# The LSTM's second step on row pairs by seven products instead of eight, and a longer stated time for the norm behind layer 2

## The chip, the cores and the metric

The kernel runs on one core of one Trainium2 chip. The metric is device time in microseconds (us) of one execution, as the median of several runs. TensorE (PE in the profile; PEld is its loading of weights), VectorE (DVE), ScalarE (ACT), GpSimd (POOL) and SyncE (SP, here only a queue that issues DMAs) each work through a list of instructions of their own, in the order in which the program was built.

## The reference

The input `x` is 128 graphs of 64 nodes with 256 features. Four graph layers follow one another, each as `x = layernorm(x + layer(x))`. Cut to what matters:

```
layer 0:  three times  adj^2 (elementwise) @ (h @ W), relu between
layer 1:  U @ (relu((U.T @ x) @ W1 + b1) @ W2 + b2),  U the eigenvectors of adj's Laplacian
layer 2:  h = relu(adj @ (x @ Wg0 + bg0));  h = relu(adj @ (h @ Wg1 + bg1))
          for p in 1..4:
              windows of p successive nodes; an LSTM with weights Wih[p-1], Whh[p-1] over each window
              h at the window's last node = last hidden state
layer 3:  attention over the graph's edges:  softmax(mask(h h^T)) h + b,  h = x W + b_lin
```

One LSTM step is

```
g = x_t @ Wih.T + h @ Whh.T + bias          # gates i, f, g, o of 256 each
c = sigmoid(f) * c + sigmoid(i) * tanh(g);  h = sigmoid(o) * tanh(c)
```

For p = 2 there are 32 windows in a graph and two steps. The first step has no `h` yet. The second step is what the change rewrites.

## The kernel before

**Tiles and groups.** The 8192 rows (graph and node) make 64 tiles of 128 rows, held in one buffer `X` of 64 x 256 floats in each of 128 partitions. Four tiles are a group: 8 graphs, 512 rows, 16 groups. Everything is fp32. A product of fp32 operands appears in the profile as two TensorE instructions, each with its loading of weights.

**Two phases.** Phase one runs layer 0 for all groups, two at a time; the eigenvectors of layer 1 are computed beside it on VectorE. All of `X` is loaded at the start through SP's queue. A list `norms` holds the single steps of layer 0's norm, which are handed out one after each product. Phase two (from about 860 us) runs layers 1, 2 and 3 group by group, three groups at a time (`WAYS = 3`), each at a different place.

**The order in phase two.** Only TensorE's order is laid out by hand. Every stage is a generator that issues a burst of products and yields the time from which its next burst may come. `now` is a clock that `mm` moves on by a stated time for each product. The loop at the end of the kernel takes the oldest group whose time has come; if none has, it sets `now` to the earliest time. The stated times are constants: `NORM = 5.2` behind a norm, `CELL[256] = 3.8` behind an LSTM step with 256 columns, `CONV`, `MOVE` and `SOFT` elsewhere. They wait for nothing; they only decide in which order the bursts stand. VectorE's, ScalarE's and GpSimd's orders come from the framework's scheduler. All four engines then go through their lists in order, and semaphores hold back an instruction whose operand isn't there.

**Around the change.** In `lstm` (L989 to L1057) the hidden states of layer 2 are held transposed, features in partitions, in `hT` (a buffer named `w` in the profile), with columns of 8 graphs x 64 nodes. A step at p = 2 has 8 units, two halves of 128 features for each of the gates f, i, g, o. A unit of the second step is four products of 256 columns, two with `wih` (L716, `w,wih`) and two with `whh` (`hs,whh`), added in one PSUM bank. ScalarE reads the bank with bias and tanh into `gates` (L1030). VectorE makes the cell (L1034, L1036, L1038), ScalarE its tanh (L1039), and VectorE stores the result into `hT` (L1051), or into `hs` (L1041) when another step follows. The weights of a sigmoid are folded into tanh with a factor of a half.

When `lstm` for p = 4 has ended, `layer2` turns the result back (L926, `ident,w`), adds it to `X` (L1096) and calls `norm`: statistics on VectorE (L551, L552), the root on GpSimd (L553, L554), the scaling on VectorE (L564). It is called for two tiles at a time. Layer 3 then turns `X` (L926, `ident,X`), multiplies by `dw`, turns the result (L926, `ident,w`), makes the scores (L1146), the exponentials on ScalarE (L1159), and turns them (L926, `ident,att`). A copy on ScalarE (`eT`, L1166) is the operand of the last products (`w,v`); VectorE adds them to `X` (L1176), and a norm and the output's DMA (L1184) follow. Layer 1 uses `u2`, `bw1`, `ut2` and `bw2` as weights and L965, L971, L986 on VectorE. Layer 2's mixing and its two products are `adT2`, `cw0`, `cw1`, with copies L953 (VectorE), L954 (ScalarE) and the addition L1067.

The last two groups (`ENDING`) are handled apart: their norms are scaled on ScalarE, and their layer 3 goes in halves.

Of the kernel before, what the change touches and what calls it, by code (L numbers as in the profile page):

```python
# [533 lines left out]
P = 128  # L534
# [3 lines left out]
ENDING = (14, 15)  # L538
LEAD = 10


def norm_parts(tc, pool, x, half, scalar=False):

# [53 lines left out]
def kernel(  # L597
# [48 lines left out]
        nc.sync.dma_start(t, src.rearrange(pattern, **kw))  # L646
        return t

    X = keep.tile([P, NT, D], F32, name="X")
    adst = keep.tile([P, N], F32, name="adst")  # L650
    eig_c = ea.tile([P, len(CONSTS), N], F32, name="eig_c")
    nc.scalar.dma_start(adst[:N, :], adj)
    nc.sync.dma_start(adst[N:, :], adj)
    nc.scalar.dma_start(X[:, 2:4, :], x_t[:, 2:4, :])
    for t in range(2):
        nc.sync.dma_start(X[:, t, :], x_t[:, t, :])
    aw1 = load(wa, "aw1", a_w1, "(k p) f -> p k f", [P, 2, 512], p=P)
    aw2 = wa.tile([P, 4, 1024], F32, name="aw2")
    for h in range(2):
        cols = slice(h * 512, (h + 1) * 512)  # L660
        nc.sync.dma_start(aw2[:, :, cols], a_w2.rearrange("(k p) f -> p k f", p=P)[:, :, cols])
    aw3 = load(wa, "aw3", a_w3, "(k p) f -> p k f", [P, 8, D], p=P)
    for t in range(4, NT, 2):
        nc.sync.dma_start(X[:, t:t + 2, :], x_t[:, t:t + 2, :])
    nc.sync.dma_start(eig_c, consts)

    ident = keep.tile([P, P], F32, name="ident")
# [74 lines left out]
            yield now[0] + 0.3  # L742

    def layer0(g):
        xs = X[:, 4 * g:4 * g + 4, :]

        def mixed(dst, src, nf, more, then=None):
            for c in range(nf):
# [105 lines left out]
        for t in (2, 0):  # L854
            p = tl(psa, [P, 2, D], "ps", bufs=6)
            mm(p, sqT2, s3[:, t:t + 2, :])
            yield now[0]
            x2 = xs[:, t:t + 2, :]
            VL.tensor_add(x2, p, x2)
            norms.extend(scalar_norm(tc, small, x2, half, spare))  # L860

# [48 lines left out]
    for i in range(4):  # L912
        wih.append(load(wb, f"wih{i}", c_ih[i], "(k p) f -> p k f", [P, 2, 1024], p=P))
        whh.append(load(wb, f"whh{i}", c_hh[i], "(k p) f -> p k f", [P, 2, 1024], p=P) if i else None)
    att = []
    for i in range(WAYS):
        att.append(wb.tile([P, 4, P], F32, name=f"att{i}"))
# [44 lines left out]
    def layer1(xs, ready):  # L962
# [25 lines left out]
            yield now[0]  # L988
        return ready  # L989

    def lstm(hT, p, first, nw):

        n = 8 * nw
        wi, wh, bias = wih[p - 1], whh[p - 1], cbi[:, p - 1, :]
        c = hs = None
        for t in range(p):
            rows = slice(first + t, first + t + (nw - 1) * p + 1, p)
            xt = [hT[:, k, rows, :] for k in range(2)]  # L1000
            last = t == p - 1
            names = "figo" if t else "igo"
            G = tl(pg, [P, 2048], "gates")[:, :2 * len(names) * n].rearrange("p (q h n) -> p q h n", h=2, n=n)
            gate = {q: G[:, i] for i, q in enumerate(names)}
            units = [(h, q) for h in range(2) for q in names]

            ahead = {}
            early = units[:2] if t else []
            for h, q in early:
                m = slice(("ifgo".index(q) * 2 + h) * P, ("ifgo".index(q) * 2 + h + 1) * P)  # L1010
                ahead[h, q] = pp = ps4()[:, :n]
                for k in range(2):
                    mm(pp, wi[:, k, m], xt[k], k == 0, False)
            if t:
                yield ready
            if p > 1 and not t:
                c = tl(pg, [P, 512], "c")[:, :2 * n].rearrange("p (h n) -> p h n", h=2)
            new = None if last else tl(pg, [P, 512], "hs")[:, :2 * n].rearrange("p (h n) -> p h n", h=2)
            for h, q in units:
                j = 2 * "ifgo".index(q) + h  # L1020
                m = slice(j * P, (j + 1) * P)
                pp = ahead.get((h, q))
                if pp is None:
                    pp = ps4()[:, :n]
                    for k in range(2):
                        mm(pp, wi[:, k, m], xt[k], k == 0, k == 1 and not t)
                if t:
                    for k in range(2):
                        mm(pp, wh[:, k, m], hs[:, k, :], False, k == 1)
                S.activation(gate[q][:, h, :], pp, AF.Tanh, bias=bias[:, j:j + 1], scale=0.5 if q == "g" else 0.25)  # L1030
                if q == "g":
                    to = gate["g"][:, h, :] if t or p == 1 else c[:, h, :]
                    if t:
                        V.scalar_tensor_tensor(c[:, h, :], gate["f"][:, h, :], 1.0, c[:, h, :], op0=ALU.add,  # L1034
                                               op1=ALU.mult)
                    V.scalar_tensor_tensor(to, gate["i"][:, h, :], 1.0, gate["g"][:, h, :], op0=ALU.add, op1=ALU.mult)  # L1036
                    if t:
                        V.scalar_tensor_tensor(c[:, h, :], c[:, h, :], 0.5, to, op0=ALU.mult, op1=ALU.add)  # L1038
                    S.activation(gate["i"][:, h, :], c[:, h, :] if p > 1 else to, AF.Tanh, scale=0.5)  # L1039
                if q == "o" and not last:  # L1040
                    V.scalar_tensor_tensor(new[:, h, :], gate["o"][:, h, :], 1.0, gate["i"][:, h, :], op0=ALU.add,  # L1041
                                           op1=ALU.mult)
                if q == "o":
                    if h == 0:
                        yield now[0]
                elif h == 1 or len(units) == 8:
                    yield now[0]
            if last:

                for h in range(2):  # L1050
                    V.scalar_tensor_tensor(hT[:, h, slice(first + p - 1, first + nw * p, p), :],  # L1051
                                           gate["o"][:, h, :].rearrange("p (w b) -> p w b", b=8), 1.0,
                                           gate["i"][:, h, :].rearrange("p (w b) -> p w b", b=8), op0=ALU.add,
                                           op1=ALU.mult)
            ready = now[0] + CELL[n]
            hs = new
        return ready  # L1057

    def layer2(xs, g, ready):
        a = yield from mixed(xs, adT2, ready)  # L1060
        g1 = as3(work(), 4)
        ready = []
        for t in range(0, 4, 2):
            p = ps4((P, 2, D))
            for j in range(2):
                run(p[:, j, :], [(a[:, k, (t + j) * P:(t + j + 1) * P], cw0[:, k, :]) for k in range(2)])
            V.tensor_add(g1[:, t:t + 2, :], p, wide["c_b0"].unsqueeze(1).to_broadcast([P, 2, D]))  # L1067
            relu(g1[:, t:t + 2, :], g1[:, t:t + 2, :])
            ready.append(now[0] + CONV)
            yield now[0]  # L1070
        a = yield from mixed(g1, adT2, ready)
        hT = tl(pw, [P, 1024], "w").rearrange("p (k n b) -> p k n b", k=2, b=8)
        for c in range(2):
            p = ps4((P, 4, P))
            run(p, [(cw1[:, k, c * P:(c + 1) * P], a[:, k, :]) for k in range(2)])
            h = work2()
            V.scalar_tensor_tensor(as3(h, 4), rs_row.unsqueeze(1).to_broadcast([P, 4, P]), cb1[:, c:c + 1], p,
                                   op0=ALU.mult, op1=ALU.add)
            S.activation(hT[:, c, :, :].rearrange("p n b -> p b n"), as3(h, 8), AF.Relu, scale=2.0)
            yield now[0]  # L1080
        ready = now[0] + CONV
        for p, first, nw in ((1, 0, 32), (1, 32, 32), (2, 0, 32), (3, 0, 21), (4, 0, 16)):
            if first == 0:
                yield ready
            ready = yield from lstm(hT, p, first, nw)
        hb = as3(work(), 2)
        V.tensor_copy(as3(hb[:, 0, :], 8), hT[:, 0, :, :].rearrange("p n b -> p b n"))
        S.copy(as3(hb[:, 1, :], 8), hT[:, 1, :, :].rearrange("p n b -> p b n"))
        yield ready + 1.6
        ready = []  # L1090
        for t in range(0, 4, 2):
            p = ps4((P, 2, D))
            for j in range(2):
                for k in range(2):
                    turn(p[:, j, k * P:(k + 1) * P], hb[:, k, (t + j) * P:(t + j + 1) * P])
            V.scalar_tensor_tensor(xs[:, t:t + 2, :], p, 0.5, xs[:, t:t + 2, :], op0=ALU.mult, op1=ALU.add)  # L1096
            norm(xs, t, ready, 1.8 if t and g in ENDING else 0.0, scalar=g in ENDING)
            yield now[0]
        return ready

# [84 lines left out]
            yield now[0]  # L1185

    def group(g):
        xs = X[:, 4 * g:4 * g + 4, :]
        ready = [0.0, 0.0]
        ready = yield from layer1(xs, ready)  # L1190
        ready = yield from layer2(xs, g, ready)
        if g in ENDING:

            mine = next(x for x in going if x[3] == g + 1)
            going.append([ready[1], mine[1] + 1, layer3(xs, g, ready, 2, 2), g + 1])
            yield from layer3(xs, g, ready, 0, 2)
        else:
            yield from layer3(xs, g, ready, 0, 4)

# [60 lines left out]
```

## Time and profile before

| | |
|---|---|
| median of 10 runs | 2539.27 us (2537.01 to 2541.73) |
| the profiled execution's own time | 2537.25 us |
| its span, first to last instruction | 2535.5 us |
| granted TensorE clock, mean | 0.997 |
| TensorE busy | 2490.7 us, 15020 instructions |
| VectorE busy | 1410.2 us, 4996 instructions |
| ScalarE busy | 1096.1 us, 2706 instructions |
| GpSimd busy | 133.1 us |
| second-step products at p = 2 with `whh` (128x256) | 512 instructions |
| VectorE busy in 0 to 800 us / 900 to 1000 us / 1000 to 2300 us | 641.6 / 31.3 / 604.2 us |

A busy time is a sum over the instructions of an engine; the profiled time is a little longer than the span, since it takes in what lies around the first and last instruction. The profile gives every instruction its line in the kernel, its output and its operands; products issued through `mm` all have the line L716, and so are told apart by their operands' names. A time of a TensorE product in the timeline ends with the model of its pipeline, so that neighbouring rows overlap; the distance of the starts says how fast products follow one another. In a table by stretches of time the columns are the stretch, its length, the busy time and number of instructions of PE, PEld, DVE, ACT and POOL, the granted clock, the share of DMA and GB/s.

### The profile page before, as it was taken

How to read it: one execution, taken by the hardware profiler on the slowest of the kernel's cores; microseconds unless marked ns; L12 is line 12 of the kernel's file. 1: busy time of each engine (PE TensorE's matmuls, PEld its weight loads, DVE VectorE, ACT ScalarE, POOL GpSimd, SP SyncE). 2: the span in 40 equal slices, each digit the busy share in tenths (PEclk: the TensorE clock that was granted, in tenths of full speed). 3: DMA queues.
4: the chain of work that ended last, by engine and by line, in shares of the span. 5: the costliest groups of instructions: out<-in, count | busy, mean ns of one | idle time of the engine just before them, and what ended most of it. 6: DMA issues, size and time to landing. Idle time of an engine off the chain costs nothing.

```text
span 2535.5 us, 38990 instructions
## 1 busy us (share of the span) xinstructions
PE 2490.7 (98%) x15020; PEld 2188.2 (86%) x15020; DVE 1410.2 (56%) x4996; ACT 1096.1 (43%) x2706; POOL 133.1 (5%) x316
## 2 busy tenths in 40 slices
PE   9999999999999999999999999999999999999997
PEld 7788887888877889998989889898898988988996
DVE  6888777778885433454453544535445444353235
ACT  2344433434333354445444454443444444445444
POOL 0000000000000100000000000000000000010001
PEclk9999999999999999999999999999999999999998
DMA  6000000000000300000000000000000000000000
GB/s 220 1 1 1 1 1 1 1 1 1 1 1 1 117 1 1 9 9 1 9 9 1 9 1 9 9 1 9 1 9 9 1 9 5 5 9 1 1 1 26
DMA packets 24634, 32.09 MB, mean 13 GB/s; under 512 B 2176, under 2 KB 21376, under 8 KB 24448
## 3 DMA queue, kind: packets, MB, share of 16 engines
q1 hardware_dynamic: 24096, 29.32, 3.4%
q8 instruction: 118, 1.93, 0.3%
q14 instruction: 68, 0.56, 0.1%
q10 hardware_dynamic: 352, 0.28, 0.0%
HBM read 21.20 MB, written 8.39 MB: 12 GB/s over the span
## 4 chain that ended last, share of the span: by engine, by line
PE 92%; DVE 5%; POOL 1%; issue 1%; DMA 1%; ACT 0%; SPq 0%; ACTq 0%; POOLq 0%; DVEq 0%
PE ps L716 89%; PE ps L926 2%; POOL ln_rs L554 1%; DVE D L51 1%; DVE X L564 1%; DVE X L1096 1%; PE ps L1146 1%; DVE ln_st L551 1%; PE pc L93 1%; DMA X<-in_x_dram 1%; DVE tw L51 0%; POOL ln_rs L553 0%; DVE ln_mv L552 0%; DVE h L51 0%; DVE u L51 0%
## 5 line engine op out<-in xcount | busy, mean ns | idle before, releaser
L716 PE MATMUL ps<-w,wih 128*128 128x256 f32 (+2 forms) x4992 | 895.3, 319 | 0.0
L716 PEld LDWEIGHTS ps<-w,wih 128*128 128x128 f32 x4992 | 761.3, 191 | 54.1 <-issue 12.7
L1030 ACT ACTIVATE gates<-ps,cbi 128x128 f32<-128x128 f32 (+2 forms) x1248 | 502.7, 410 | 574.1 <-PE ps L716 567.0
L716 PE MATMUL ps<-hs,whh 128*128 128x128 f32 (+2 forms) x3072 | 539.7, 303 | 0.8 <-DVE hs L1041 0.8
L716 PEld LDWEIGHTS ps<-hs,whh 128*128 128x128 f32 x3072 | 453.0, 191 | 17.2 <-issue 1.7
L1036 DVE SCALAR_TENSOR_TENSOR gates<-gates 128x256 f32<-128x256 f32 (+2 forms) x256 | 89.5, 349 | 294.6 <-ACT gates L1030 294.6
L716 PE MATMUL ps<-aw,h 128*128 128x256 f32 x1024 | 227.2, 379 | 0.0
L716 PEld LDWEIGHTS ps<-aw,h 128*128 128x128 f32 x1024 | 192.9, 190 | 25.9 <-ACT h L725 0.5
L725 ACT ACTIVATE h<-h 128x512 f32<-128x512 f32 x128 | 80.6, 629 | 169.4 <-DVE h L51 169.2
L1039 ACT ACTIVATE gates<-c 128x128 f32<-128x128 f32 (+2 forms) x288 | 98.0, 340 | 94.0 <-DVE c L1038 83.4
L1034 DVE SCALAR_TENSOR_TENSOR c<-gates,c 128x128 f32<-128x128 f32 (+2 forms) x192 | 62.6, 326 | 117.8 <-ACT gates L1030 117.5
L716 PE MATMUL ps<-ss,tw 128*128 128x256 f32 x512 | 117.9, 380 | 0.0
L716 PE MATMUL ps<-ss,aw 128*128 128x256 f32 x512 | 117.3, 379 | 0.0
L716 PE MATMUL ps<-m,aw 128*128 128x256 f32 x512 | 117.1, 380 | 0.0
L716 PE MATMUL ps<-aw,m 128*128 128x512 f32 x256 | 114.5, 593 | 0.0
L1041 DVE SCALAR_TENSOR_TENSOR hs<-gates 128x128 f32<-128x128 f32 (+2 forms) x192 | 62.7, 327 | 89.2 <-ACT gates L1039 51.6
L564 DVE TENSOR_SCALAR X<-X,ln_mv,ln_rs 128x256 f32<-128x256 f32 x176 | 64.8, 410 | 81.0 <-POOL ln_rs L554 81.0
L1051 DVE SCALAR_TENSOR_TENSOR w<-gates 128x256 f32<-128x256 f32 (+2 forms) x160 | 59.5, 378 | 90.2 <-PE ps L716 61.0
L716 PEld LDWEIGHTS ps<-ss,aw 128*128 128x128 f32 x512 | 96.6, 190 | 12.8
L716 PEld LDWEIGHTS ps<-ss,tw 128*128 128x128 f32 x512 | 96.3, 190 | 12.9 <-issue 0.2
L553 POOL TENSOR_SCALAR ln_rs<-ln_mv 128x2 f32<-128x2 f32 x96 | 25.4, 264 | 1555.7 <-DVE ln_mv L552 1555.3
L716 PEld LDWEIGHTS ps<-m,aw 128*128 128x128 f32 x512 | 95.6, 190 | 12.6 <-issue 0.5
(294 smaller groups left out, 3089.3 us busy)
## 6 DMA issues: line engine op xcount, KB each, us to landing
X<-in_x_dram SPq DMA_DIRECT2D x30, 256.0 KB, 6.0
out_dram<-X SPq DMA_DIRECT2D x28, 256.0 KB, 2.1
wih<-in_c_ih_dram SPq DMA_DIRECT2D x4, 1024.0 KB, 7.2
aw<-in_a_w_dram SPq DMA_DIRECT2D x3, 1024.0 KB, 10.3
whh<-in_c_hh_dram SPq DMA_DIRECT2D x3, 1024.0 KB, 9.3
out_dram<-X SPq DMA_DIRECT2D x8, 128.0 KB, 1.7
aw<-in_a_w_dram SPq DMA_DIRECT2D x1, 512.0 KB, 5.8
cw<-in_c_w_dram SPq DMA_DIRECT2D x2, 256.0 KB, 5.1
```

The source lines that it names most:

```text
L51: return getattr(self.engine, name)(out, *args, **kw)
L553: nc.gpsimd.tensor_scalar(rs, mv[:, :, 1], EPS, None, op0=ALU.add)
L564: nc.vector.tensor_scalar(x[:, t, :], x[:, t, :], mv[:, t, 0:1], rs[:, t:t + 1], op0=ALU.subtract, op1=ALU.mult)
L716: PE.matmul(out, lhsT, rhs, start=start, stop=stop)
L725: S.activation(dst, src, AF.Relu)
L926: PE.transpose(out, in_, ident)
L1030: S.activation(gate[q][:, h, :], pp, AF.Tanh, bias=bias[:, j:j + 1], scale=0.5 if q == "g" else 0.25)
L1034: V.scalar_tensor_tensor(c[:, h, :], gate["f"][:, h, :], 1.0, c[:, h, :], op0=ALU.add, op1=ALU.mult)
L1036: V.scalar_tensor_tensor(to, gate["i"][:, h, :], 1.0, gate["g"][:, h, :], op0=ALU.add, op1=ALU.mult)
L1039: S.activation(gate["i"][:, h, :], c[:, h, :] if p > 1 else to, AF.Tanh, scale=0.5)
L1041: V.scalar_tensor_tensor(new[:, h, :], gate["o"][:, h, :], 1.0, gate["i"][:, h, :], op0=ALU.add, op1=ALU.mult)
L1051: V.scalar_tensor_tensor(hT[:, h, slice(first + p - 1, first + nw * p, p), :], gate["o"][:, h, :].rearrange("p (w b) -> p w b", b=8), 1.0, ...
```

## The change

It has three parts.

1. **The norm behind layer 2** is given a stated time that is longer by 1.3 for all groups but the last two.
2. **The second step at p = 2** goes through a new function `second`. The 32 windows are split into two halves of 16, the 256 input features (partition halves) and the 1024 gate rows into two each, and the 2 x 2 block product is made from seven block products by Strassen's scheme in Winograd's form, once with `wih` and `xt` and once with `whh` and `hs`, both added in the same place in PSUM. `less` makes four combinations of the moving operand for each of `xt` and `hs` on VectorE; `add_weights` makes four combinations of each weight once, in the first group. A product P1 to P7 is two units (`q`) of 128 columns, 4 TensorE products each; two products P share a PSUM bank. ScalarE copies P1 to `u1`, and VectorE adds the others into the four blocks a, b, c12 and d of the gates. ScalarE then applies bias and tanh from there, two windows' halves in one instruction, and the stores into `hT` come at the end of the step's function, four pieces of 128 columns in place of two of 256.
3. **Room for the sums.** The two buffers of weight sums take 16 KB in each partition. `X` is cut to 48 tiles. The last four groups go through layer 0 first. Their rows are stored in DRAM (`rest`) when their norm is done, and the space is loaded with the rows of groups 0 to 3. When groups 0 to 3 have left layer 3, the stored rows are loaded back. The store and the two loads are one more entry in the list `norms` for each of the four groups.

```diff
@@ load, layer0 @@
-    X = keep.tile([P, NT, D], F32, name="X")
+    X = keep.tile([P, NT - 4 * LATE, D], F32, name="X")
+    rest = [aside.tile([P, 4, D], F32, name=f"rest{i}") for i in range(LATE)]
+    order = list(range(NT // 4 - LATE, NT // 4)) + list(range(NT // 4 - LATE))
...
+        def change():
+            nc.sync.dma_start(rest[g], xs)
+            for t in (0, 2):
+                nc.sync.dma_start(xs[:, t:t + 2, :], given(order[g + LATE])[:, t:t + 2, :])
...
+        if g < LATE:
+            norms.append(change)
@@ weights @@
+    def add_weights():
+        for w, s in zip((wih[1], whh[1]), sums):
+            a11, a12, a21, a22 = quarters(w)
+            V.tensor_add(s[:, 0], a21, a22)
+            V.tensor_sub(s[:, 1], s[:, 0], a11)
+            V.tensor_sub(s[:, 2], a11, a21)
+            V.tensor_sub(s[:, 3], a12, s[:, 1])
@@ new: second @@
+    def second(hT, xt, hs, G, c, bias, ready):
+        def less(s, b1, b2, part):
+            T = [both[:, s, i].rearrange("p (w b) -> p w b", b=8) for i in range(4)]
+            if 0 in part:
+                V.tensor_sub(T[0], b1[1], b1[0])
+            if 1 in part:
+                V.tensor_sub(T[2], b2[1], b1[1])
+                V.tensor_sub(T[1], b2[1], T[0])
+                V.tensor_sub(T[3], b2[0], T[1])
...
+        less(0, x1, x2, (0, 1))
+        less(1, h1, h2, (0, 1))
...
+        moving = ((x1[0], h1[0]), (x2[0], h2[0]), (x2[1], h2[1]), T4, T1, T2, T3)
+        weight = (0, 1, 6, 2, 3, 4, 5)
+        yield ready
+        for h in range(2):
...
+            def two(*which):
+                p = ps4((P, 2, 2, P))
+                for at, i in enumerate(which):
+                    for q in range(2):
+                        for s in range(2):
+                            mm(p[:, at, q, :], ways[s][weight[i]][:, q, h, :], moving[i][s], s == 0, s == 1)
+                return p[:, 0], p[:, 1]
+
+            p1, p2 = two(0, 1)
+            S.copy(u1, p1)
+            V.tensor_add(a, u1, p2)
+            yield now[0]
+            p6, p7 = two(5, 6)
+            V.tensor_add(c12, u1, p6)
+            V.tensor_add(b, c12, p7)
+            yield now[0]
+            p5, p3 = two(4, 2)
+            V.tensor_add(d, b, p5)
+            V.tensor_add(c12, c12, p5)
+            V.tensor_add(c12, c12, p3)
+            p4, _ = two(3)
+            V.tensor_add(b, b, p4)
+            gate = {}
+            for m, q, name in ((1, 0, "f"), (0, 0, "i"), (0, 1, "g"), (1, 1, "o")):
+                j = 2 * "ifgo".index(name) + h
+                gate[name] = G[:, h, :, m, q, :]
+                S.activation(gate[name], gate[name], AF.Tanh, bias=bias[:, j:j + 1],
+                             scale=0.5 if name == "g" else 0.25)
+            ch = c[:, h, :].rearrange("p (w n) -> p w n", w=2)
+            V.scalar_tensor_tensor(ch, gate["f"], 1.0, ch, op0=ALU.add, op1=ALU.mult)
+            V.scalar_tensor_tensor(gate["g"], gate["i"], 1.0, gate["g"], op0=ALU.add, op1=ALU.mult)
+            V.scalar_tensor_tensor(ch, ch, 0.5, gate["g"], op0=ALU.mult, op1=ALU.add)
+            S.activation(gate["i"], ch, AF.Tanh, scale=0.5)
+            yield now[0]
+        for h in range(2):
+            for w in range(2):
+                o, i = (G[:, h, w, m, 0 if m == 0 else 1, :].rearrange("p (w b) -> p w b", b=8) for m in (1, 0))
+                V.scalar_tensor_tensor(hT[:, h, 32 * w + 1:32 * w + 32:2, :], o, 1.0, i, op0=ALU.add, op1=ALU.mult)
+        return now[0] + CELL[256] + 1.0
@@ lstm @@
+            if p == 2 and t:
+                ready = yield from second(hT, xt, hs, G, c, bias, ready)
+                break
@@ layer2 @@
+            elif g == 0:
+                add_weights()
...
-            norm(xs, t, ready, 1.8 if t and g in ENDING else 0.0, scalar=g in ENDING)
+            norm(xs, t, ready, 1.8 if t and g in ENDING else 0.0 if g in ENDING else 1.3, scalar=g in ENDING)
@@ group @@
+        if g < LATE:
+            nc.sync.dma_start(xs, rest[g])
```

## The prediction

> **What bounds the kernel now.** I read the page's busy shares first, then TensorE's list of waits, then two neighbouring groups in the timeline, then the table by stretches. Times are us; in the list of waits the figures are total, times, longest.
>
> ```profile
> PE 2490.7 (98%) x15020; PEld 2188.2 (86%) x15020; DVE 1410.2 (56%) x4996; ACT 1096.1 (43%) x2706; POOL 133.1 (5%) x316
> ...
> PE ps L926 <- DVE X L564: 17.1, 22, 1.1
> ```
>
> TensorE bounds: 98% busy, and its one repeated wait is that of layer 3's transposes (L926) for the norm behind layer 2 (L564), 22 times, so in 11 groups of 16. One such place, TensorE and then VectorE:
>
> ```profile
> 1500.93 1.89 PE L716 MATMUL ps<-w,wih 128*128 128x256 f32 x8
> 1502.65 1.05 PE L716 MATMUL ps<-ut,v 128*128 128x128 f32 x8
> 1504.80 0.67 PE L926 MATMUL ps<-ident,X 128*128 128x128 f32 x4 [1.09 <-DVE X L564]
> 1505.30 1.03 PE L716 MATMUL ps<-bw,v 128*128 128x256 f32 x4
> 1506.80 0.76 PE L926 MATMUL ps<-ident,X 128*128 128x128 f32 x4 [0.47 <-DVE X L564]
> 1507.46 2.86 PE L716 MATMUL ps<-w,wih 128*128 128x256 f32 x12
> ...
> 1569.13 3.73 PE L716 MATMUL ps<-w,wih 128*128 128x128 f32 x32
> 1572.70 1.95 PE L716 MATMUL ps<-bw,w 128*128 128x128 f32 x16
> ```
>
> ```profile
> 1504.24 0.74 DVE L564 TENSOR_SCALAR X<-X,ln_mv,ln_rs 128x256 f32<-128x256 f32 x2 [0.81 <-POOL ln_rs L554]
> 1505.04 0.40 DVE L1036 SCALAR_TENSOR_TENSOR gates<-gates 128x256 f32<-128x256 f32 x1
> 1506.34 0.74 DVE L564 TENSOR_SCALAR X<-X,ln_mv,ln_rs 128x256 f32<-128x256 f32 x2 [0.90 <-POOL ln_rs L554]
> 1506.99 0.75 DVE L1051 SCALAR_TENSOR_TENSOR w<-gates 128x256 f32<-128x256 f32 x2
> ```
>
> A row can be used by its starts: eight instructions of 256 columns take 1502.65-1500.93, 0.215 each; 32 of 128 columns take 1572.70-1569.13, 0.1116 each. The last turn of layer 2 leaves TensorE at 1500.93 and layer 2's next step, the first of row pairs (wih1, 1507.46), starts 6.53 later over 4.36 of products: 2.2 of idle time in a group. And wih1 starts when L1051 has written half of its input (1506.99+0.42). So two things are late together: the norm, and this LSTM input queued behind it on VectorE.
>
> The stretches, columns PE, PEld, DVE, ACT, POOL busy:
>
> ```profile
> 1500.93:1507.46 6.53, 4.97 (x30) 3.84 (x29) 4.82 (x17) 1.95 (x4) 1.92 (x4) 1.00 0.00 0
> 1507.46:1540.52 33.06, 33.06 (x193) 28.02 (x193) 20.98 (x57) 12.60 (x26) 3.92 (x8) 1.00 0.05 17
> 1540.52:1604.00 63.48, 63.48 (x461) 60.27 (x460) 21.44 (x61) 32.50 (x87) 0.00 (x0) 1.00 0.01 1
> ```
>
> VectorE's 56% is a mean over two regimes. In the 39.6 from layer 2's turns to step p=3 (layer 3 of one group, row pairs of the second, layer 1 of the third) it is busy 25.8, and sits six times 0.75 to 1.13 for GpSimd's root; in the 63.5 after that, 21.4.
>
> [...] The rows here have 423 (L971, from PSUM) and 292 (L1041, another operation). [...]
>
> **The change, part by part.** Where instructions stand in the changed program is read from its built order; all durations are from this trace.
>
> *Strassen's products.* Removed per group: 32 fp32 products of 256 columns, two instructions each, 64 x 0.2155 = 13.8. Added: 7 products x 2 x 2 x 2 halves = 56 of 128 columns, 112 x 0.1116 = 12.5. Gain 1.3 a group, 21.0 in 16.
>
> *Its additions.* VectorE gets 14 from PSUM (423 ns) and 8 of 128 columns (292), and the results are stored in 4 pieces of 128 instead of 2 of 256 (+0.3): 5.9+2.3+0.3 = 8.6 busy a group, or 6.4 where nothing depends (rows follow at 0.335 and 0.21). ScalarE gets two copies (0.37 each, L1120's). All 8.6 lies in the busy stretch: 25.8+8.6 = 34.4, with the six waits for GpSimd 40.0, over TensorE's 36.1. Its cover is gone.
>
> *The stated time* (+1.3). In ten groups the order after the turns becomes wih0, ut2, bw2, X turns, wih1 (6 products), X turns. VectorE's order there is unchanged: norm of the first rows, L1036, norm of the second, LSTM input. So wih1 still waits for L1051's place, 6.45 after the turns, with 0.44 less done ahead of it. The wait for L564 should go, and a wait of wih1 for the LSTM input (1.8), with 0.6 of bw2 for ScalarE's copy, takes its place: no gain, 0.44 lost.
>
> *A steady group,* walked from wih1's start (0) by starts and ends of such rows, every engine in its built order:
>
> ```
>  9.9  PE: layer 1's last product done (2.6 wih1 + 0.4 turns + 2.6 wih1 + 3.5 dw + 0.9)
> 13.6  DVE: its add, statistics, 1.15 for GpSimd, norm
> 17.4  DVE: a=u1+P2, two hn adds, scores, c12=u1+P6
> 19.1  DVE: exp on ACT (to 18.4), sums of rows
> 20.4  DVE: b+P7, d=b+P5, c12+P5, b+P4, c12+P3 -> ACT f,i,g,o to 21.85
> 22.8  ACT: second copy of P1, then eT; PE wanted eT at 22.2: waits 0.6
> 31.3  DVE: cell, h, attention added, two norms with 1.1 for GpSimd each
> 31.9  DVE: copy for cw0; PE wanted it at 30.8: waits 1.2
> 32.7  DVE: b, d, c12 of the second half -> ACT to 34.4
> 35.5  DVE: cell, mixed with two layer-1 adds and a copy; ACT tanh to 36.0
> 36.65 DVE: h stored. PE wanted it for p=3 at 33.7: waits 3.0
> ```
>
> Against 33.06 now: +3.6 a group, that is 4.8 of waits, 0.4 of the moved turns, less 1.3 and some rounding. Behind the waiting rows on VectorE stand the norms and adds of the other two groups, and TensorE, in its fixed order, waits for them.
>
> *Elsewhere.* In the first three groups and the last three, 5 to 8 us of other products lie between the last P4 and p=3, or bursts of other steps between the products: I take 1 each for waits, bounds 0 and 3.5 (the steady sum). The sums of weights are 8 operations of 512 columns, 8 x 0.68 = 5.5 on VectorE in the first group, where TensorE is idle 4.1 in 850 to 900: 2 taken, bounds 0 and 5.5. Bank releases: every PSUM bank's eighth predecessor is read before it is wanted.
>
> *Rows kept aside.* SP stores four groups (512 KB each) and loads as much, in layer 0 and again behind the outputs. A 256 KB load lands in 6.0 and a store in 2.1; the store stands behind the norm (about 100 us for the first group, or one group later), and the next reader comes after another group of products, about 50 us. Behind it on SP are only the weights of layer 2, issued 500 us later. The reloads are wanted eight groups later. Cost 0; without that cover some 10 us each.
>
> *Sum:* -21.0 + 10 x 4.9 + 6 + 2 = +36 on the profiled execution's 2537.25: 2573. The median shown is 2.0 above it: **2575**.
>
> **Rivals.**
> - *VectorE keeps up* (faster). If the additions slip into gaps, the 4.8 of new waits vanish and -21+4+6+2 = -9 is left; if the norm's waits also go (11 x 2.2), -37: 2502 to 2530. For it: 56% mean, and at the short spacing the additions are 6.4, not 8.6. Against: six waits for GpSimd block that queue. It decides where the waits of a steady group fall below some 1.2.
> - *Half of it.* With VectorE's chain 2 shorter (dependent rows closer, attention's adds ahead), waits are about 2.8: +16, 2555; with 3.5 shorter, no change.
> - *It spreads.* If the late h delays p=3's first gates and the next norms too, 2 more a group: 2595, up to 2606.
> - *The order change isn't what it says*: the built order shows it made, but a burst moved ahead of a wait has to be ready itself, and wih1 isn't.
>
> **Numbers.** A measurement of this kernel tells about 0.2% (5 us) from no change. Main case 0.62, 2560 to 2590. Half of it 0.11, spreading 0.12, no change 0.05, faster 0.10. The range 2545 to 2606 leaves out the last two and a little above. Slower 0.85.
>
> **What would show it.** Right: waits of L926 for the norm nearly gone; TensorE waiting instead for LSTM inputs (hT) at wih1 and wih2 and for cw0's copy, 60 to 80 in all; VectorE busy near 34 of a stretch of 43; matmul spacing still 0.1116. Wrong: TensorE without waits in p=2 (then the additions were hidden), or waits for DMA or in layer 0.

## The result, and the profile after

| | before | after |
|---|---|---|
| median | 2539.43 us (28 runs) | 2582.46 us (8 runs) |
| ratio, 95% interval | | 1.0169 (1.016 to 1.0178) |
| span of the profiled execution | 2535.5 us | 2579.6 us |
| mean granted clock | 0.997 | 0.992 |

The changed kernel is slower by 43 us; 2575 was predicted. The page's first line of busy times, as shown for the kernel before:

```profile
PE 2490.4 (97%) x15788; PEld 2211.3 (86%) x15788; DVE 1520.1 (59%) x5388; ACT 1097.2 (43%) x2738; POOL 139.7 (5%) x316
```

TensorE has 768 instructions more and is busy as long as before. VectorE has 110 us more; without the wide sums of the weights (5.4) that is 6.5 a group. The time went into TensorE's waits (total, times, longest):

```profile
PE ps L731 <- DVE w L1104: 20.0, 9, 2.2
PE ps L731 <- DVE w L1171: 15.0, 10, 1.5
PE ps L731 <- DVE w L997: 9.3, 10, 1.9
PE ps L731 <- ACT v L1023: 9.1, 12, 1.4
PE ps L731 <- DVE hs L1161: 5.7, 2, 4.9
```

The wait for layer 2's norm (17.1 before) has gone. In its place TensorE waits for the hidden states of p = 2 at the first products of p = 3 (wih2, for L1104), for those of p = 1 at wih1 (L1171), for the copy in front of cw0 (L997) and for ScalarE's copy in front of bw2 (L1023). This is the place behind layer 2's turns, to be read beside the one at 1500.93 in the prediction, TensorE and then VectorE:

```profile
1519.15 1.89 PE L731 MATMUL ps<-w,wih 128*128 128x256 f32 x8
1520.88 1.05 PE L731 MATMUL ps<-ut,v 128*128 128x128 f32 x8
1522.61 1.13 PE L731 MATMUL ps<-bw,v 128*128 128x256 f32 x4 [0.68 <-ACT v L1023]
1523.58 0.60 PE L970 MATMUL ps<-ident,X 128*128 128x128 f32 x4
1525.68 2.86 PE L731 MATMUL ps<-w,wih 128*128 128x256 f32 x12 [1.50 <-DVE w L1171]
```

```profile
1522.46 0.73 DVE L566 TENSOR_SCALAR X<-X,ln_mv,ln_rs 128x256 f32<-128x256 f32 x2 [0.81 <-POOL ln_rs L556]
...
1524.56 0.73 DVE L566 TENSOR_SCALAR X<-X,ln_mv,ln_rs 128x256 f32<-128x256 f32 x2 [0.90 <-POOL ln_rs L556]
1525.21 0.75 DVE L1171 SCALAR_TENSOR_TENSOR w<-gates 128x256 f32<-128x256 f32 x2
```

The turns of `X` find the norm done and start without a wait, but wih1 behind them needs L1171, which still stands behind both scalings and their waits for GpSimd's root. And this is the end of the second step in the same group, all engines, few rows of many:

```profile
1552.62 0.39 PE L731 MATMUL ps<-w,whh 128*128 128x128 f32 x2
...
1553.02 0.74 DVE L566 TENSOR_SCALAR X<-X,ln_mv,ln_rs 128x256 f32<-128x256 f32 x2 [0.75 <-POOL ln_rs L556]
...
1556.02 0.73 DVE L566 TENSOR_SCALAR X<-X,ln_mv,ln_rs 128x256 f32<-128x256 f32 x2 [0.82 <-POOL ln_rs L556]
...
1557.28 0.41 DVE L1086 TENSOR_TENSOR gates<-gates,ps 128x256 f32<-128x256 f32 x1
...
1557.60 0.41 DVE L1088 TENSOR_TENSOR gates<-gates,ps 128x256 f32<-128x256 f32 x1
...
1561.36 0.49 DVE L1104 SCALAR_TENSOR_TENSOR w<-gates 128x128 f32<-128x128 f32 x2
...
1561.91 6.22 PE L731 MATMUL ps<-w,wih 128*128 128x168 f32 x30 [2.22 <-DVE w L1104]
```

The last P4 is done at 1552.85, where TensorE's next row starts. Its addition (L1088) starts 4.75 later, behind layer 3's attention, its norm and two pairs of scalings that waited for GpSimd. Gates, cell and stores follow, and hT is there at 1561.85, 9.0 after P4. The program stated 4.8 for it.

The two stretches of this group (from layer 2's turns to p = 3, and most of the rest; columns PE, PEld, DVE, ACT, POOL busy, then granted clock, DMA share, GB/s):

```profile
1519.01:1561.91 42.90, 37.66 (x274) 32.93 (x272) 33.08 (x98) 14.84 (x33) 5.58 (x12) 1.00 0.04 14
1561.91:1625.61 63.70, 63.70 (x450) 60.70 (x451) 20.33 (x59) 31.26 (x84) 0.00 (x0) 0.97 0.00 1
```

In the first VectorE is busy 33.1 of 42.9 and TensorE 37.7. The second row stops 1.8 short of the next group's wih0, which starts at 1627.42. From wih0 to wih0 the two stretches are 42.8 and 65.5, where the kernel before has 39.6 and 64.0 (1540.52 to 1604.54). In the second TensorE has no wait, but a granted clock of 0.97: a loss of another kind, told below.

**Where the 44.1 of the span lie,** by the starts of the groups' `w,dw` products (once a group):

| from the start of ... | before | after | difference |
|---|---|---|---|
| the span to the 1st group | 1018.3 | 1024.4 | +6.1 |
| 1st to 4th | 284.6 | 293.8 | +9.2 |
| 4th to 13th, nine steps | 932.5 | 964.4 | +31.9 |
| 13th to 14th, with the last groups between | 234.5 | 230.1 | -4.4 |
| 14th to the end | 65.5 | 66.9 | +1.4 |

A step of the nine is 106.6 against 103.6, and 108.3 in three of them.

### The profile page after: what moved, and what is told of

Same layout as the page of the kernel before. It is cut to its first block, busy times and chain, and to the rows that moved or that the text cites. A ratio compares the mean times of both kernels' runs of the same rounds, so it can differ in the third digit from the quotient of the medians.

```text
span 2579.6 us, 41027 instructions
## 1 busy us (share of the span) xinstructions
PE 2490.4 (97%) x15788; PEld 2211.3 (86%) x15788; DVE 1520.1 (59%) x5388; ACT 1097.2 (43%) x2738; POOL 139.7 (5%) x316
## 4 chain that ended last, share of the span: by engine, by line
PE 81%; DVE 12%; POOL 3%; ACT 2%; issue 2%; DMA 0%; SPq 0%; ACTq 0%; POOLq 0%; DVEq 0%
PE ps L731 79%; POOL ln_rs L556 2%; DVE X L566 2%; DVE ln_st L553 2%; PE ps L970 1%; ACT gates L1093 1%; DVE D L51 1%; POOL ln_rs L555 1%; DVE X L1218 1%; DVE ln_mv L554 1%; PE pc L93 1%; DVE w L1262 1%; DMA X<-in_x_dram 0%; DVE X L1298 0%; DVE w L997 0%
## 5 line engine op out<-in xcount | busy, mean ns | idle before, releaser
L731 PE MATMUL ps<-w,wih 128*128 128x128 f32 (+2 forms) x4864 | 848.3, 311 | 35.7 <-DVE w L1104 20.0
L731 PEld LDWEIGHTS ps<-w,wih 128*128 128x128 f32 x4864 | 730.4, 193 | 75.2 <-DVE w L1104 22.3
L1150 ACT ACTIVATE gates<-ps,cbi 128x128 f32<-128x128 f32 (+2 forms) x1120 | 440.7, 403 | 450.7 <-PE ps L731 444.4
L731 PE MATMUL ps<-hs,whh 128*128 128x128 f32 (+1 forms) x2816 | 459.6, 287 | 5.7 <-DVE hs L1161 5.7
L731 PEld LDWEIGHTS ps<-hs,whh 128*128 128x128 f32 x2816 | 397.3, 192 | 9.0 <-DVE hs L1161 6.1
L1156 DVE SCALAR_TENSOR_TENSOR gates<-gates 128x128 f32<-128x128 f32 (+2 forms) x224 | 75.9, 339 | 245.5 <-ACT gates L1150 245.4
L740 ACT ACTIVATE h<-h 128x512 f32<-128x512 f32 x128 | 80.5, 629 | 183.9 <-DVE h L51 183.8
L1161 DVE SCALAR_TENSOR_TENSOR hs<-gates 128x128 f32<-128x128 f32 (+2 forms) x192 | 62.7, 327 | 93.9 <-ACT gates L1159 58.9
L731 PE MATMUL ps<-w,sums 128*128 128x128 f32 x896 | 114.1, 276 | 0.0
L1159 ACT ACTIVATE gates<-c 128x128 f32<-128x128 f32 (+2 forms) x256 | 84.5, 330 | 62.7 <-DVE c L1158 48.1
L731 PEld LDWEIGHTS ps<-w,sums 128*128 128x128 f32 x896 | 107.4, 192 | 1.7 <-issue 0.5
L1154 DVE SCALAR_TENSOR_TENSOR c<-gates,c 128x128 f32<-128x128 f32 (+1 forms) x160 | 49.2, 307 | 100.5 <-ACT gates L1150 99.9
```

The costliest lines, as they stand in the source:

```text
L731: PE.matmul(out, lhsT, rhs, start=start, stop=stop)
L740: S.activation(dst, src, AF.Relu)
```

## Experiments

All ratios are to the kernel before on the same chip, with a 95% interval.

### The parts alone

e1, in the kernel before:

```diff
-norm(xs, t, ready, 1.8 if t and g in ENDING else 0.0, ...)
+norm(xs, t, ready, 1.8 if t and g in ENDING else 0.0 if g in ENDING else 1.3, ...)
```

> The kernel before with the norm's stated time longer by 1.3 and nothing else. VectorE's queue is the bound (the theory): the wait for the norm gives place to one of the LSTM input at wih1, no gain and up to 0.44 a group lost in ten groups: 2538 to 2546 against 2539. Rival, the order of bursts does the harm: 2560 or more. Rival, the norm's wait really goes: some 2519 (11 x 1.8 less).

Measured: 2536.63, ratio 0.9990 (0.9983 to 0.9996). A small gain, below the expected range: the groups now come in steps of 107.4 and 98.2 by turns, where both kernels' steps are even but for the clock. TensorE's order is thus another one than the changed kernel's, and e1 doesn't tell what the stated time does in that order.

e2, in the changed kernel, with the norm's stated time of before:

```diff
-            if p == 2 and t:
-                ready = yield from second(hT, xt, hs, G, c, bias, ready)
-                break
```

> The changed kernel with the second step in its old form and the norm's stated time as before: only the rows kept in DRAM and the sums of weights (which nothing reads) are left of the change. Theory: 2 more than before, 2539 to 2544, all of it about 880 to 900 us, where the eight wide additions stand. Rival, the DRAM traffic or the placement costs: 2550 or more, with waits for DMA.

Measured: 2542.67, ratio 1.0008 (1.0002 to 1.0015), some 2 to 3. No wait for the added DMAs. Instead one wait of 4.1 for `w` of L740 at about 890, where the kernel before had 1.2 and 1.4: on VectorE layer 2's first addition stands behind five of the eight wide sums. A stretch of 6.8 at half the granted clock begins at 889, which the kernel before doesn't have. The storing and loading of rows costs nothing that shows.

e5, in the changed kernel, puts the norm's stated time back (the diff of e1 reversed):

> The changed kernel with the norm's stated time of before. If the waits of wih1 (1.5) and of the product behind ScalarE's copy (0.68) come from the longer stated time, they go, and the wait for the norm comes back (1.09 and 0.47 a group): about 0.6 a group less, 2572 to 2582. If the two parts harm each other, clearly less: below 2565. If the norm's waits are longer now that VectorE has more to do: 2585 or more.

Measured: 2548.93, ratio 1.0039 (1.0024 to 1.0054): 33 less than the changed kernel. The outcome is the second of the expectation: **the two parts harm each other.** Alone the stated time gains 3; beside the second step it costs 33. With its old value the second step costs 6 over e2: 27 are lost where 21 are saved. Here too the steps come by turns (108.4 and 98.6 to 101.2), so this one number changed the whole order. And between 900 and 2460 e5 ran 27 us at half the granted clock, some 14 of the 27 that are lost; e2 ran none there (mean granted clock of the profiled executions 0.989 and 0.995).

### Is it VectorE's load?

e3 leaves the additions and the copies of P1 out of the changed kernel; the gates are read from the banks:

```diff
-            S.copy(u1, p1)
-            V.tensor_add(a, u1, p2)
...
-            V.tensor_add(b, b, p4)
...
-                S.activation(gate[name], gate[name], AF.Tanh, ...
+                S.activation(gate[name], (p4 if m else p2)[:, q, :].unsqueeze(1).to_broadcast([P, 2, P]), AF.Tanh, ...
```

> The changed kernel without its 14 additions from PSUM per group and without the copies of P1: ScalarE reads its gates from the banks of P2 and P4 direct, so the values are wrong, all seven products and the eight combinations of the moving side stay. VectorE loses 5.9 of the 8.6 us that it gained. Theory, VectorE: the waits for hT at wih1, wih2 and for cw0's copy mostly vanish, 2500 to 2530. Rival, TensorE's halved products or the order cost it: still above 2560.

Measured: 2539.67, ratio 1.0003 (0.9995 to 1.0012). All of the 43 goes, which speaks against the rival that the halved products or the order do it without the additions, but 2500 to 2530 is missed, and the waits say why:

```profile
PE ps L731 <- DVE w L1161: 15.0, 10, 1.5
PE ps L731 <- ACT v L1023: 8.0, 12, 1.0
PE ps L731 <- DVE w L997: 6.0, 9, 0.7
```

(L1161 here is L1171 of the changed kernel.) The wait at wih2 is gone; in a steady group those at wih1 (1.50) and bw2 (0.68) are what they were, and that for cw0's copy is a little shorter. So the wait at wih2 comes with the additions, and those at wih1 and bw2 don't need them; e9 below shows that they go with another order. The early wait for `hs` (4.9) is there without the additions too. A step is 103.7: the 1.3 saved in products is lost in these.

e4 puts as many additions, into a scratch buffer, into e2, without e2's sums of the weights:

```diff
+            if p == 2 and t:
+                for k in range(8):
+                    V.tensor_sub(extra[:, :P], hs[:, k % 2, :P], hs[:, k % 2, P:])
...
+                if p == 2 and t:
+                    for _ in range(1 + (h == 0 or q in "fi")):
+                        V.tensor_add(extra, hs[:, h, :], pp)
                 S.activation(gate[q][:, h, :], pp, AF.Tanh, ...
```

> The kernel of e2 with its old products (without the sums of weights), and on VectorE 14 additions of 256 columns from the PSUM banks of the second step and 8 of 128 columns, all into a scratch buffer that nothing reads: the load of the change, on nobody's data path. Theory, VectorE's queue: waits of TensorE for hT, for the norm and for copies grow by some 3 to 5 a group, 2570 to 2610. Rival, it is the longer path from the products to the gates (P4 behind two additions) and not the load of the queue: below 2550.

Measured: 2555.92, ratio 1.0065 (1.005 to 1.008), 13 over e2, or some 16 if the 2 to 3 for e2's wide sums are taken off; it lies between the two expectations. One new wait (cw0's copy, 12.0 in 10 times); a step is 105.0. VectorE was as busy as in the changed kernel (1520.4). So in the order of before the load by itself costs 1.4 in a steady group and 13 to 16 in all, about what e5 loses beyond the clock (27 less 14). Whether the rest of the changed kernel's loss comes from its order alone, or also from additions that stand on the way from the products to the gates, e4 can't say: it differs from the changed kernel in both.

e6 takes layer 3's scaling off that queue, in the changed kernel, and e11 does the same in the kernel before:

```diff
-            rows_norm(tc, small, x2, half, ending)
+            rows_norm(tc, small, x2, half, True)
```

> The changed kernel with the scaling of layer 3's norm on ScalarE in all groups, as in the last two. It takes four scalings and two waits for GpSimd's root (0.8 each), 3.1 in all, out of VectorE's queue, just where the additions of the second half stood 4.4 behind the last P4. Theory, these additions wait their turn in that queue: wih2's wait of 2.22 falls below 0.7, and with it the half-clock stretches in the middle go; 2550 to 2562. Rival, the tail from P4 over two additions, four gates and the cell is too long by itself: wih2 still waits 1.5 or more, above 2572.

> The kernel before with the scaling of layer 3's norm on ScalarE: the control for the gain of 27 in the changed kernel. Theory, it is the additions that stand behind these scalings, and the kernel before has none: 2534 to 2542. Rival, a norm off VectorE's queue helps any order: below 2525.

Measured: e6 2555.20, ratio 1.0064 (1.0047 to 1.0081), 27 less than the changed kernel; e11 2540.08, ratio 1.0000 (0.9992 to 1.0009). The same edit is worth 27 where the additions stand behind the scalings and nothing where there are none. The end of the second step in e6, TensorE's last P4 and VectorE, whose other rows are left out:

```profile
1542.29 0.39 PE L731 MATMUL ps<-w,whh 128*128 128x128 f32 x2
```

```profile
1543.30 0.41 DVE L1088 TENSOR_TENSOR gates<-gates,ps 128x256 f32<-128x256 f32 x1
1543.63 0.41 DVE L1086 TENSOR_TENSOR gates<-gates,ps 128x256 f32<-128x256 f32 x1
...
1549.04 0.49 DVE L1104 SCALAR_TENSOR_TENSOR w<-gates 128x128 f32<-128x128 f32 x2
```

P4 ends at 1542.52, and its addition starts 0.8 behind it instead of 4.75; hT is stored at 1549.53, 7.0 after P4, and wih2 waits no more. The rival (the tail is too long by itself) falls: a tail of 7.0 is hidden by the products that lie there. The half-clock stretches between 1130 and 2460 are gone too (mean granted clock 0.995, the changed kernel's 0.992). The price is a new wait for ScalarE's copy in front of cw0 (L998, 11.6 in 10 times), about as long as the one for VectorE's copy that went; a step is 104.7.

e7 moves layer 1's and layer 2's scalings to ScalarE too:

```diff
-            norm(xs, t, ready, 2.0)
+            norm(xs, t, ready, 2.0, True)
...
-            norm(xs, t, ready, ..., scalar=g in ENDING)
+            norm(xs, t, ready, ..., scalar=True)
```

> As the last, with the scalings of layer 1's and layer 2's norms on ScalarE too. VectorE then waits for GpSimd nowhere in the stretch. Theory: the waits at wih1, wih2 and cw0's copy all shrink, 2515 to 2550. Rival, ScalarE takes the place of VectorE (its gates queue behind scalings that wait for the root): above 2560, with waits for ScalarE's outputs.

Measured: 2599.58, ratio 1.0238 (1.0223 to 1.0254). The rival is right here:

```profile
PE ps L731 <- ACT v L1023: 51.1, 12, 5.0
```

ScalarE's copy for bw2 now stands behind scalings that wait for GpSimd, and TensorE waits some 4.8 for that copy in a steady group. Each of these waits in a steady group is followed by 6.8 at half the granted clock, another 3.4 (mean granted clock 0.983). A wait for another engine was paid by what stood behind it, in ScalarE's queue as in VectorE's.

### Is it the order?

e9, in the changed kernel, states 7.0 in place of 4.8, nearer to the 9.0 that the trace shows:

```diff
-        return now[0] + CELL[256] + 1.0
+        return now[0] + CELL[256] + 3.2
```

> The changed kernel with one number changed: the stated time behind the second step, from 3.8 + 1.0 to 3.8 + 3.2. The trace of the changed kernel has 9.0 from the last P4 to the stored hT. The order that is built has the second half of cw0's products ahead of p = 3's first step, and the input products of p = 1 ahead of the turns of layer 2. Theory, the harm is a lack of other products where VectorE is behind, which the order decides: wih2's wait of 2.22 falls by 1.7 or more, and wih1 has its input earlier: 2530 to 2560. Rival, VectorE's load of the stretch is what counts and the waits only move to other bursts: above 2570.

Measured: 2537.84, ratio 0.9991 (0.9983 to 1.0000), **45 less than the changed kernel**, with the same work on every engine. Two rows of TensorE at the turns and three around p = 3:

```profile
1514.28 4.48 PE L731 MATMUL ps<-w,wih 128*128 128x256 f32 x20
1518.60 0.60 PE L970 MATMUL ps<-ident,X 128*128 128x128 f32 x4
...
1547.16 3.72 PE L731 MATMUL ps<-cw,w 128*128 128x256 f32 x16 [0.84 <-DVE w L997]
1550.72 0.45 PE L731 MATMUL ps<-w,wih 128*128 128x168 f32 x2
1551.66 4.54 PE L731 MATMUL ps<-w,wih 128*128 128x168 f32 x30 [0.50 <-DVE w L1104]
```

The second half of cw0's products now lies ahead of p = 3 (16 instructions in place of 8), and wih1 ahead of the turns of `X`. In a steady group the waits at wih1 and bw2 are gone, that at wih2 is 0.5, that for cw0's copy is still 0.84. The last P4 is done at 1542.59, so hT comes about as late as before, some 9 after P4: the longer tail is still there, but products cover it. A step is 102.6.

e10 has the norm's stated time of before and e6's edit:

> The kernel with the norm's stated time of before (2549) and the scaling of layer 3's norm on ScalarE (which took 27 in the other order). Theory, VectorE's queue: the waits for cw0's copy (10.9 in all) shrink, 2530 to 2543. Rival, the order there has its products elsewhere and nothing waits behind layer 3's scalings: 2546 or more.

Measured: 2527.51, ratio 0.9948 (0.9933 to 0.9963), below the expected range: the scalings off the queue are worth 21 in that order too, and the result beats both kernels.

e12 takes e9 and scales layer 3's norm on GpSimd, right behind the root in the same queue, in all groups but the last two:

```diff
-        nc.vector.tensor_scalar(x[:, t, :], ...
+        (nc.gpsimd if pool_scales else nc.vector).tensor_scalar(x[:, t, :], ...
...
-            rows_norm(tc, small, x2, half, ending)
+            rows_norm(tc, small, x2, half, ending, not ending)
```

> The kernel with the later stated time behind the second step (2538), and layer 3's norm scaled on GpSimd itself, behind its root, in all groups but the last two; TensorE's order stays. VectorE loses four scalings a group and its two waits for those roots, and ScalarE gets nothing. Theory, VectorE's queue: the remaining 0.84 for cw0's copy and 0.5 for hT fall to 0.3 or less each, and less stands ahead of the early wait for hs (4.9): 2518 to 2530. Rival, GpSimd's scalings are long (none of this size is in a trace so far), and the next root on GpSimd queues behind them, or they slow VectorE: 2538 or more.

Measured: **2512.16, ratio 0.9889 (0.9873 to 0.9906)**, below the expected range. From 1200 to 2300, TensorE's whole list of waits is

```profile
PE ps L731 <- ACT v L740: 2.5, 10, 0.3
PE ps L731 <- ACT v L1023: 1.0, 1, 1.0
PE ps L731 <- ACT w L1199: 0.7, 1, 0.7
PE ps L731 <- DVE w L997: 0.4, 1, 0.4
```

and a step is 100.8, which is 103.6 less the 1.3 of the products and the 1.6 of waits that the kernel before had. The price on GpSimd (columns: count, busy, mean ns):

```profile
L566 POOL TENSOR_SCALAR X<-X,ln_mv,ln_rs 128x256 f32<-128x256 f32 x56 | 72.9, 1309 | 3.0
```

1.31 for one scaling by the profile, three times VectorE's 0.41. No wait of TensorE names these scalings. The rival's later roots aren't seen either: the scalings left on VectorE wait 52.2 for GpSimd's root in 60 times, against 74.3 in 88 in e9, so some 0.85 each in both. The kernel before with its scalings on GpSimd was not run; with them on ScalarE (e11) it gained nothing.

### The clock

e8, in the changed kernel, fills the wait at wih2 with useless products:

```diff
                     pp = ps4()[:, :n]
+                    if p == 3 and not t and (h, q) == units[0]:
+                        for _ in range(8):
+                            PE.matmul(pp[:, :P], ident, ident, start=True, stop=True)
```

> The changed kernel with eight useless products (the identity by itself, 16 instructions of 128 columns, 1.8) ahead of the first product of p = 3, where TensorE waits 2.22 for hT. Nothing else moves. If a wait of 2.2 makes the granted clock fall to a half for 3.41 in those groups where it lies in one period of a fixed grid: three of the six such stretches go, 3 x 1.7 less, 2575 to 2579, for more work. If the clock falls for another reason: 2581 to 2586, or more where the products aren't hidden.

Measured: 2583.02, ratio 1.0171 (1.0156 to 1.0186): no change in the sum, which lies in the range of the expectation's rival. By parts both signs are there: the nine steps are all 106.6 (959.4 instead of 964.4, the 5 expected), with no stretch at half clock in them (mean granted clock 0.995); but groups in which TensorE doesn't wait at p = 3 pay the 1.8 in full (13th to 14th: 235.5 instead of 230.1, three times 1.8), which the expectation had left out. The link of wait and clock holds in the nine steps; the total was worked out wrong.

## Why the prediction was right

**The mechanism** was that of the main case: VectorE's additions sit in the stretch where its queue has little room, the norm's wait turns into waits for LSTM inputs, and TensorE, in a fixed order, waits. In a steady group, with the prediction's steps:

| wait for | predicted | measured |
|---|---|---|
| ScalarE's copy, at bw2 | 0.6 | 0.68 |
| LSTM input, at wih1 | 1.8 | 1.50 |
| eT, at `w,v` | 0.6 | none |
| copy, at cw0 | 1.2 | 0.83 |
| hT, at wih2 | 3.0 | 2.22 |
| a steady group against before | +3.6 | +3.0, and +0.5 by the clock |

VectorE's 34 of 43 came as 33.1 of 42.9. The spacing of the products stayed: ten of 128 columns from 1550.17 to 1551.28, 0.111 each. The gain of 21 is thus real, and e12, whose step is shorter than before's by the 1.3 and by the norm's wait, collects it.

**Terms that were off.** The additions were given 8.6 of VectorE's time a group and took 6.5, close to the 6.4 that the prediction had for rows that don't depend on each other. The walk made the new waits too long, wih2's by 0.8 and eT's by 0.6, and the waits at wih1, wih2 and for cw0's copy, which were to be 60 to 80 in all, came to 44; a restart behind a wait costs a little more than the wait (the products of cw0 start 0.99 after those before them are through by their spacing, for 0.83 shown), which gave back part of it. The fall of the granted clock was not in the sum at all: about 12 of the 44 (below). It made the kernel slower than the sum, where the waits that were taken too long had made the sum too large. The wide sums were given 2 (0 to 5.5) and measured 2 to 3 in e2, with the half clock behind them. The first three steps were given -0.3 each, as having products enough, and came out at +9.2: they hold a wait of 4.9 for `hs` at 1136, where the first products of p = 3 are followed by only 1.8 of others, one of 1.9 for cw0's copy, and two stretches at half clock. The end, given the same, came out at -3.0. That the total is off by only 7 is in part luck: waits that were smaller were made up by the clock and by the first groups.

**The step that explains less than it seemed** is that of the stated time: "no gain, 0.44 lost". In the steady group it holds: 1.56 of the norm's wait went, and 1.50 and 0.68 came. But it looks at one place in one order, and the number moved the whole order: without the new second step it gains 3 (e1), with it it costs 33 (e5). The loss of 43 needs two causes together: changing the order (e5, e9), or leaving out the additions or freeing VectorE's queue ahead of them (e3, e6), takes most of it away. The prediction put it down to VectorE's additions in one given order, without a price for the order; e4 has their load at 13 to 16 in the order of before.

**The rivals.** "VectorE keeps up" was priced at 2530, and at 2502 if the norm's waits go as well, to be decided where a steady group's waits fall below 1.2. The changed kernel has 5.2 and is slower; e9 has 1.6 and is the same as before within 0.2%; e12 has 0.25 and is faster by 1.1%. The case was a real one: one stated number and four scalings a group decided against it. "It spreads" isn't seen: the nine steps are alike but for the clock.

What stays open: the wait of 4.9 at 1136 was read from the order and not tried on its own. It is 4.9 without the additions (e3) and in e9, 2.9 in e6, 2.0 in e12 and at most 1.6 in e5, so neither the additions nor the second step's stated time account for it. And how much of the loss comes from the additions' place between products and gates, apart from order and load, was not separated.

## What to carry to other kernels

An instruction between two engines takes on the lateness of its queue (27 us here, e6 against the changed kernel): before putting an addition between products and gates, look at what stands ahead of it there, above all at instructions that wait for a third engine; a scaling that nobody is waiting for belongs on another engine or behind. Where bursts are ordered by stated times, a rewritten step needs its time read anew from a trace (9.0 here against 4.8 stated): stating 7.0 was worth 45 us, twice the products that were saved. The mean share of an engine (VectorE's 56%) says nothing on the stretch that decides (33.1 of 42.9 in the changed kernel, with waits for GpSimd besides).

## What the hardware showed that was not expected

A short wait can cost more than itself. The half-clock stretches in the middle of the changed kernel start at 1136.44, 1238.84, 1563.10, 1778.14 and 2099.00. Each lasts 3.413, and the starts are 30, 95, 63 and 94 times 3.413 apart, so in this trace they lie on one grid of windows of that length. Four of these windows, two around each of two equal waits of 2.22 at wih2 (first busy column PE, granted clock third from the end):

```profile
1559.69:1563.10 3.41, 1.19 (x8) 1.19 (x9) 2.16 (x6) 1.67 (x5) 0.00 (x0) 1.00 0.00 0
1563.10:1566.51 3.41, 3.41 (x14) 3.41 (x13) 0.67 (x2) 1.67 (x5) 0.00 (x0) 0.50 0.00 0
1665.50:1668.91 3.41, 2.28 (x10) 1.82 (x10) 3.41 (x9) 2.17 (x5) 0.00 (x0) 1.00 0.23 77
1668.91:1672.33 3.42, 2.15 (x15) 2.15 (x16) 1.55 (x5) 2.26 (x6) 0.00 (x0) 1.00 0.02 5
```

The first wait lies in one window, which is idle for 2.2 of 3.4, and the next window runs at half clock: from 1563.20 to 1566.28 its instructions of 168 columns start 0.280 apart, where those before and behind it start 0.142 apart, and by that some 1.7 us are lost. The second wait is shared by two windows with 1.1 and 1.3, and nothing follows. So an equal wait costs 2.2 or, by this working, 3.9, by where it falls. Over the changed kernel between 900 and 2460, every window with 2.0 or more of idle time was followed by half a clock and none with 1.86 or less; between these both happened (1.89 was followed by it, 1.96 was not). The lower figure is this kernel's alone: in e10 TensorE waits 1.81 for cw0's copy four times, and the 32 instructions of 168 columns that come next take 6.46 and 5.76 behind two of these waits (those that end at 1432.91 and 1843.38) and 4.85 behind the two others (1638.95 and 2049.18). How the clock weighs a partly idle window stays open. Five such stretches and a longer one at 890.7 (6.8) make some 12 us. The kernel before, with no wait above 1.1 between 900 and 2500, had no such stretch there.

GpSimd's scalings of 128x256 (1.31 each) ran beside VectorE without slowing it in what could be compared: in e12 VectorE's additions at L1088, one of which runs from 1531.31 beside a pair of scalings from 1530.78 to 1533.21, took 414 ns in the mean of 32, and in e9, where GpSimd scales nothing, 413.
